# Attention and ternary feed-forward in one kernel: the values by seven products, the chains in twos, two row normalisations on ScalarE, and an earlier decision between paths

## The chip, the cores and the metric

The program runs on one core of a Trainium2 chip. The metric is the time of one execution on the device in microseconds: 1585.0 us as the median of three runs (1584.58 to 1585.37) for the kernel before.

## The reference: what is computed

The input x has 8 sequences of 512 tokens with 256 features, all in f32. Two layers follow each other, each added to its input.

```python
x = x + layernorm(attention(layernorm(x)))
x = x + layernorm(ffn(layernorm(x)))

# attention: 16 heads of 64
q = l2norm(heads(x @ w_q)) * exp(scale)
k = l2norm(heads(x @ w_kv[:, :1024]))
v = heads(x @ w_kv[:, 1024:])
out = merge(softmax(q @ k.T) @ v) @ w_out + b_out

# feed-forward: w1, w2: 256 -> 1024, h1, h2: 1024 -> 1024, w3: 1024 -> 256, entries -1, 0 or 1
h = silu((x @ w1.T) * s1) * ((x @ w2.T) * s2)
h = gelu((h @ h1.T) * hs1)
h = gelu((h @ h2.T) * hs2)
y = (h @ w3.T) * s3
```

## The kernel before

**Order.** Nothing is issued as it is written. Every piece of work is a step with an engine, an estimated length, what it reads and writes and which buffers it takes (`Steps.add`, line 54). `Steps.issue` (line 84) then plays the steps through: TensorE's steps keep the order in which they were added, and each other engine (VectorE, ScalarE, GpSimd, SyncE with its DMA queue) takes, of the steps that are ready by the estimates, the one with the earliest due time. The outcome is the fixed instruction order of every engine. One such plan covers attention, a second one the feed-forward part. On the chip each engine runs its list in order and waits at whatever is not ready.

**Attention.** A batch (one sequence) has 16 heads in two halves of 8 (`hf`), and 8 units, one for each pair of heads. A unit makes four score steps (`scores`, line 728: keys on partitions, two heads at once in the upper and lower rows of the array), eight exponentials on ScalarE, three sums of the exponentials over key blocks on VectorE (`summed`, tile `es`), and four value steps (`values`, line 782, tile `po`, the two heads in the two column halves). The value steps of a unit run after the scores of that unit and before those of the next. For two units together, `row_sums` (tile `pd`) gives the softmax denominators, which go through a fold, a reciprocal and a spread by DMA (`inverted_two`, line 847) before VectorE scales the outputs `oT`.

**Projections beside the units.** The queries, keys and values of the next batch or half are made between the units. The string list `BESIDE` (line 974) has one entry for each of the 8 units: c is a link of a q or k chain, v a value step, x the normalisation and transposes of 128 rows of the next batch, t the sums of token halves, q and k the norm products, m the key norms' transposes, o one output projection, l the store and reload of rows. The products of these stand in TensorE's order between a unit's scores and the next unit's values (q and k ahead of the scores).

A *v step* (`v_step`, line 714, by `projected`, line 400) multiplies 128 tokens by 512 columns of the value weights in two products (two blocks of 128 input features), and ScalarE copies the result to the tile `v`. Four of them make a half.

A *chain* (`qk_chain`, line 518) makes a half of q or k with seven quarter products in place of eight, by the Strassen-Winograd scheme over (2 feature blocks) x (2 halves of 256 columns) x (2 halves of 256 tokens). Its seven links are one product pair each: `product` adds two 256-wide matmuls, `kept` copies a running sum out of its PSUM bank on ScalarE, `added` adds a bank into the tile on VectorE, and `squared` makes the squares for the norms. Links share three banks, so a link that goes on adding in a bank waits until that bank's earlier sum was read. The sums of weight quarters are made once (`qk_weight_sums`, line 482), those of tokens once a batch (`token_sums`, line 498). Batch 0 has all its projections made directly at the start (`qk_step`, `v_step`).

**The weight check.** The fast path is right only if the feed-forward weights are -1, 0 or 1 and the score bound holds. During attention, `looked_at` (line 1077) loads weight rows of 1024 columns into the pool `wp` (two buffers) and VectorE marks and gathers deviations into the tile `loose`, 512 columns at a time; `weight_sums` (line 1114) makes four sums of weight blocks for the square layers and stores them to DRAM. `at(...)` in line 1166 names the slots (two for each unit) where this work is added.

**Feed-forward.** Batches go in pairs through `gated`, two square layers (`square`, line 1479, seven products of quarter size with the activations split in two parts) and `ffn_out` (line 1599). There each 128 rows y are scaled, get mean and variance on VectorE, a power on GpSimd (`power`, line 313), are normalised and added to x1 on VectorE (`added`, line 1641), and stored. The rows y live in the pool `rows`, four buffers of the tag a. The first batch's rows get the same treatment at the start in `norm_in` (line 338).

**The decision.** Lines 1715 to 1723, after all steps, reduce `loose` and the bound to one number by a small product over the partitions (tile `pm_bits`), and all engines load it; a nonzero value starts a second, slower program (`tile_row_softmax`). With these inputs it isn't run.

## Time and profile before

| What | Value |
|---|---|
| Median of three runs | 1585.0 us |
| The profiled execution's own time | 1584.32 us |
| Its span, first to last instruction | 1582.5 us |
| Mean granted TensorE clock | 0.998 |
| TensorE busy with matmuls | 1564.5 us (99%) |
| VectorE, ScalarE, GpSimd busy | 1059.5, 917.6, 486.6 us |
| Products of the v steps (line 407) | 256 records, 120.6 us busy |
| Links of the q and k chains (line 539) | 784 records |
| First projection of batch 0 (line 433) begins | 8.23 us |
| First scores (line 738) begin | 55.22 us |
| Last product of the output layer ends | 1571.63 us |
| Last add on VectorE (line 1645) | 1575.93 to 1576.36 us |

All views come from one profiled execution, with times from its span's start. A group's line names the source line, the engine, the operation, the tiles it writes and reads, its shape and count, then the busy time, the mean duration in ns and the engine's idle time before it with what ended it. A line of the timeline has start, duration, engine and line; the count behind x is of merged instructions. Matmuls overlap by a little, so the distance between two starts is what a piece of work costs. Attention ends and the feed-forward part begins at about 980 us.

### The profile page before, as it was taken

The page shows a single profiled execution, that of the slowest core. Times are in us where ns is not written, and L with a number is a line of the kernel's source. Part 1 is how long each engine was busy: PE and PEld are TensorE (multiplying, and loading weights), DVE is VectorE, ACT ScalarE, POOL GpSimd, SP SyncE. Part 2 cuts the span into 40 slices and gives each one's busy share as a digit, 9 for nine tenths or more (in the row PEclk, how much of TensorE's full clock was granted, in tenths as well). Part 3 has the DMA queues.
Part 4 walks back from the last instruction along what each step waited for, and adds up shares of the span by engine and source line. Part 5 has one row for each costly group of instructions (what it writes and reads, how often), then busy time and mean ns, then how long its engine had stood idle before and what let it go on. Part 6 is the DMA issues. An engine that isn't in the chain of part 4 may idle for free.

```text
span 1582.5 us, 19689 instructions
## 1 busy us (share of the span) xinstructions
PE 1564.5 (99%) x7208; PEld 996.6 (63%) x7208; DVE 1059.5 (67%) x1772; ACT 917.6 (58%) x1543; POOL 486.6 (31%) x354
## 2 busy tenths in 40 slices
PE   9999999999999999999999999999999999999997
PEld 4344554554554554554554546788888888888886
DVE  4577776786654553554544557869877886879686
ACT  4666556556556556555555553666466636655662
POOL 4212122122221221321221211554165235625451
PEclk9999999999999999999999999999999999999999
DMA  6233433342220220220221313344324523451540
GB/s 178 65 97 102 120 82 109 121 115 76 54 62 15 58 65 15 58 62 18 58 64 43 85 38 88 111 142 156 121 80 133 171 69 107 146 152 49 160 133 29
DMA packets 77829, 142.66 MB, mean 90 GB/s; under 512 B 18844, under 2 KB 34460, under 8 KB 73628
## 3 DMA queue, kind: packets, MB, share of 16 engines
q1 hardware_dynamic: 58140, 78.40, 17.9%
q0 software_dynamic: 18880, 61.87, 12.5%
q8 instruction: 58, 0.95, 0.3%
q10 hardware_dynamic: 704, 1.05, 0.2%
q14 instruction: 47, 0.39, 0.1%
HBM read 123.49 MB, written 17.29 MB: 89 GB/s over the span
## 4 chain that ended last, share of the span: by engine, by line
PE 96%; DVE 2%; DMA 1%; ACT 0%; issue 0%; POOL 0%; SPq 0%; DVEq 0%
PE g L1494 26%; PE s L738 15%; PE po L792 14%; PE pa L914 7%; PE vp L407 7%; PE p L1420 6%; PE g_q L539 5%; PE g_k L539 5%; PE py L1608 4%; PE pd L816 2%; PE pn_q L627 1%; PE pn_k L627 1%; PE kp L433 1%; PE qp L433 1%; PE pk L698 0%; DMA spread_q<-nq 0%
## 5 line engine op out<-in xcount | busy, mean ns | idle before, releaser
L749 ACT ACTIVATE e<-s,kn 128x512 f32<-128x512 f32 x512 | 306.7, 702 | 96.6 <-PE s L738 96.6
L738 PE MATMUL s<-qT,kT 64*128 64x512 f32 x1024 | 237.1, 602 | 0.0
L1494 PE MATMUL g<-h,wb_S 128*128 128x512 f32 x1024 | 234.3, 389 | 0.0
L792 PE MATMUL po<-e,v 128*64 128x512 f32 x1024 | 233.9, 598 | 0.0
L1494 PEld LDWEIGHTS g<-h,wb_S 128*128 128x128 f32 x1024 | 192.0, 188 | 39.8
L738 PEld LDWEIGHTS s<-qT,kT 64*128 64x128 f32 x1024 | 93.6, 186 | 143.2 <-issue 125.7
L1494 PE MATMUL g<-h,wb_A 128*128 128x512 f32 x768 | 176.4, 389 | 0.0
L314 POOL TENSOR_TENSOR kn<-kn,neghalf 128x32 f32<-128x32 f32 x16 | 87.5, 5468 | 285.8 <-DVE kn L702 285.8
L772 DVE TENSOR_TENSOR es<-es,e 128x1024 f32<-128x1024 f32 x128 | 156.8, 1225 | 24.9 <-ACT e L749 14.0
L1494 PEld LDWEIGHTS g<-h,wb_A 128*128 128x128 f32 x768 | 144.0, 188 | 29.7
L792 PEld LDWEIGHTS po<-e,v 128*64 128x64 f32 x1024 | 69.4, 136 | 139.7 <-issue 131.1
L1312 DVE TENSOR_TENSOR h<-C,h 128x512 fp32r<-128x512 f32 x112 | 129.4, 1211 | 3.9 <-ACT h L1302 3.8
L314 POOL TENSOR_TENSOR nf_q<-nf_q,neghalf 128x32 f32<-128x32 f32 x16 | 87.3, 5456 | 144.9 <-DVE nf_q L661 144.9
L772 DVE TENSOR_TENSOR es<-e,e 128x1024 f32<-128x1024 f32 x64 | 78.3, 1224 | 72.2 <-ACT e L749 71.9
L1312 DVE TENSOR_TENSOR h<-B,h 128x512 fp32r<-128x512 f32 x112 | 107.8, 1001 | 27.1 <-ACT h L1302 26.7
L407 PE MATMUL vp<-wv_sb,aT 128*128 128x512 f32 x256 | 120.6, 599 | 0.0
L914 PE MATMUL pa<-wo_sb,oT 128*128 128x256 f32 x512 | 116.5, 381 | 0.0
L1550 POOL TENSOR_TENSOR B<-B,B 128x512 f32<-128x512 f32 x64 | 102.0, 1621 | 38.9 <-DVE B L1451 34.0
L914 PEld LDWEIGHTS pa<-wo_sb,oT 128*128 128x128 f32 x512 | 95.8, 190 | 20.0 <-ACT e L749 6.1
L888 ACT COPY oT<-po 128x512 f32<-128x512 f32 x64 | 37.4, 584 | 120.2 <-PE po L792 118.2
L878 DVE RECIPROCAL fold<-fold 128x16 f32<-128x16 f32 x31 | 7.8, 252 | 147.0 <-DMA fold<-d 147.0
L1550 POOL TENSOR_TENSOR C<-C,C 128x512 f32<-128x512 f32 x64 | 94.0, 1495 | 27.7 <-DVE h L1312 27.2
(170 smaller groups left out, 2320.8 us busy)
## 6 DMA issues: line engine op xcount, KB each, us to landing
wb_S<-s POOLq DMA_DIRECT2D x32, 1024.0 KB, 5.1
spread_q<-nq SPq DMA_DIRECT2D x32, 512.0 KB
rden<-r SPq DMA_DIRECT2D x62, 256.0 KB
wb_A<-in_h1T_dram POOLq DMA_DIRECT2D x12, 1024.0 KB, 5.6
wb_A<-in_h2T_dram POOLq DMA_DIRECT2D x12, 1024.0 KB, 5.6
s<-w SPq DMA_DIRECT2D x32, 256.0 KB
w<-in_h1T_dram SPq DMA_DIRECT2D x8, 512.0 KB
x<-xres SPq DMA_DIRECT2D x32, 128.0 KB
```

The source lines that it names most:

```text
L314: nc.gpsimd.tensor_tensor(d, d, neghalf.to_broadcast([P, n]), ALU.pow)
L407: nc.tensor.matmul(pm, lhsT=T["aT", b][:, c, ts(t, P)], rhs=w[:, c, c0 : c0 + HALF], start=(c == 0), stop=(c == ND - 1),)
L539: nc.tensor.matmul(T[key][:, o, :], lhsT=w[:, ts(o, P)], rhs=rhs, start=(fresh and o == 0), stop=True, skip_group_check=True,)
L738: nc.tensor.matmul(tile_of(ps_w, [P, S], tags[h], ss[h]), lhsT=T[kT][hp, j, ts(jb, P)], rhs=T[qT][hp, j, :], start=True, stop=True,)
L749: nc.scalar.activation(T[e][:, h, :], T[ss[h]], AF.Exp, scale=T["kn", b, hf][:, jb, 2 * j + h : 2 * j + h + 1],)
L772: nc.vector.tensor_tensor(T[t], T["e", b, p, 0] if jb == 1 else T[t], T["e", b, p, jb], ALU.add)
L792: nc.tensor.matmul(T[po][h * DH : (h + 1) * DH, :], lhsT=T[v][:, jb, c0 : c0 + DH], rhs=T[e][:, h, :], start=(jb == 0), stop=(jb == NT - 1),)
L914: nc.tensor.matmul(T[pm], lhsT=T["oT", b, p][:, ts(t, P)], rhs=wo_sb[:, p, :], start=(p == 0), stop=(p == NP - 1),)
L1312: lambda: nc.vector.tensor_tensor(T[h][:, 1, c, :], T[raw][:, c, :], T[h][:, 0, c, :], ALU.subtract),
L1420: nc.tensor.matmul(T[ps[k]], lhsT=(w1r, w2r)[k][c][:, ts(o, P)], rhs=row_halves(b, i)[0][:, c, :], start=(c == 0 and i == 0), stop=(c == N ...
L1494: nc.tensor.matmul(T[to[o]], lhsT=T[w][:, c, ts(o, P)], rhs=T[h][:, i, c, :], start=(first and c == 0 and i == 0), stop=(c == NQ - 1 and i ...
L1550: lambda: (nc.gpsimd if T_ENGINE == "pool" else nc.vector).tensor_tensor(T[dst][:, c, :], T[x][:, c, :], T[y][:, c, :], ALU.subtract),
```

## The change

The values of batches 1 to 7 are made by the same seven-product chains as q and k: `qk_chain` becomes `qkv_chain`, where a chain for v has the tokens as the stationary operand and the weights as the moving one, keeps four sums by ScalarE and adds three by VectorE, and makes no squares. The weight sums exist for v too, and are now made after the direct projections of batch 0, whose value products read the weights that they overwrite.

`BESIDE` deals chains out in twos: in unit 0 the k chain (d) and the v chain of the second half alternate link by link, in unit 2 the q chain (c) and the k chain of the next batch's first half, in unit 6 its second half's q chain and first half's v chain. The links' order within a chain changes (the sixth after the third, the fourth after the fifth). Units 3, 4, 5 and 7 have no links.

The weight check works on 256 columns at a time, with one load buffer in place of two and loads and stores of half the width; weight blocks come in 16 pieces of two loads each.

The rows of batch 0 at the start and those of the last two batches at the end are normalised by an Identity activation on ScalarE, with a bias that VectorE makes first; the last rows y stand in one buffer of the pool `blockp` in place of four in `rows`. The decision's instructions become steps that are added ahead of the last pair's square layers.

```diff
-    wp = attn_scope.enter_context(tc.tile_pool(name="wp", bufs=2))
+    wp = attn_scope.enter_context(tc.tile_pool(name="wp", bufs=1))
...
+        if (kind, b) == ("a", 0):
+
+            nb = ("nb", *n)
+
+            def bias():
+                tile_of(small, [P, 1], "nb", nb)
+                nc.vector.scalar_tensor_tensor(
+                    T[nb], T[mv][:, 0:1], -1.0, T[rs], ALU.mult, ALU.mult
+                )
+
+            def normed_rows():
+                tile_of(rows, [P, D], "a", xn)
+                nc.scalar.activation(T[xn], T[x][:, t, :], AF.Identity, bias=T[nb], scale=T[rs])
+
+            steps.add("dve", 0.15, bias, reads=[(rs, 0)], writes=[(nb, 0)], takes=[("nb", 4, nb)])
+        steps.add(
+            "act" if (kind, b) == ("a", 0) else "dve", 0.42, normed_rows,
+            reads=[(x, t), (rs, 0), (("nb", *n), 0)], writes=[(xn, 0)], takes=[("a", 4, xn)],
...
+    wsum = qksum.tile([P, 6, 3, 2 * P], F32, name="wsum")
     HS = S // 2
 
     def quarter(which, hf, k):
-        w = wq_sb if which == "q" else wk_sb
+        w = {"q": wq_sb, "k": wk_sb, "v": wv_sb}[which]
         if k[0] == "A" or k == "S3":
             i, j = (1, 0) if k == "S3" else (int(k[1]) - 1, int(k[2]) - 1)
             return w[:, j, hf * HALF + i * HS : hf * HALF + (i + 1) * HS]
-        return wsum[:, "qk".index(which) * 2 + hf, "S1 S2 S4".split().index(k), :]
-
-    def qk_weight_sums(which, hf):
+        return wsum[:, "qkv".index(which) * 2 + hf, "S1 S2 S4".split().index(k), :]
+
+    def qkv_weight_sums(which, hf):
...
+    def qkv_chain(b, hf, which):
 
 
         n = (which, b, hf)
         to, sq, t = (which + "T", b, hf), ("spread", *n), ("tsum", b)
+        if which == "v":
+            to = ("v", b, hf)
...
+                    x_, y = (rhs, w) if which == "v" else (w, rhs)
                     nc.tensor.matmul(
-                        T[key][:, o, :], lhsT=w[:, ts(o, P)], rhs=rhs,
+                        T[key][:, o, :], lhsT=x_[:, ts(o, P)], rhs=y,
...
         def part(i, k):
+            if which == "v":
+                i, k = k, i
             return T[to][:, 2 * i : 2 * i + 2, ts(k, HS)]
+
+        own = "v" if which == "v" else which + "T"
...
+            if which == "v":
+                return
...
         def fourth():
             added(0, 1, product(3, "S4", "B22", 1, False, last=True))
+            squared(0)
 
         def fifth():
             added(1, 1, product(7, "S3", "T3", 0, False))
 
         def sixth():
             added(0, 0, product(2, "A12", "B21", 2, True, last=True))
-            squared(0)
 
         def seventh():
             kept(1, 0, product(4, "A22", "T4", 0, False, last=True))
             squared(1)
 
-        return [first, second, third, fourth, sixth, fifth, seventh]
+        return [first, second, third, sixth, fifth, fourth, seventh]
...
+            "pe", 0.86, products, reads=[(e, 0), (e, 1), (v, jb), *((v, ("c", i, jb // 2)) for i in range(2))],
+            writes=[(po, 0)],
...
-        "c c v c c c c v c x x x x",
+        "d v d v d v d v d v d v d v x x x x",
         "k o m o t",
-        "c c o c c c c o c",
-        "q v v l",
-        "c c v c c c c v c",
-        "k v",
-        "c c m c c c c v c",
+        "c d o c d o c d c d c d c d c d",
+        "q k l",
+        "m",
+        "",
+        "c v c v c v c v c v c v c v",
         "q",
...
-    loose = const.tile([P, S], I32, name="loose")
+    STRIP = 256
+    loose = const.tile([P, STRIP], I32, name="loose")
...
+            for c0, rows_of in loads:
+                shape = rows_of.shape[1:]
+                d = dst[:, c0 : c0 + shape[0] * (shape[1] if len(shape) > 1 else 1)]
+                nc.sync.dma_start(
+                    d if len(shape) == 1 else d.rearrange("p (c n) -> p c n", n=shape[1]), rows_of
+                )
...
+            "sync", 0.1 * len(loads), load, lag=9.0, writes=[(w, i) for i in range(4)],
+            takes=[("wrows", 1, w)], earliest=after,
+        )
+        for i in range(4):
...
+                "dve", 0.38, lambda i=i: marked(i), reads=[(w, i)], writes=[(y, 0)],
                 takes=[("y", 1, y)],
             )
             steps.add(
-                "dve", 0.72, lambda i=i: gathered(i), reads=[(y, 0)], writes=[("loose", 0)]
+                "dve", 0.38, lambda i=i: gathered(i), reads=[(y, 0)], writes=[("loose", 0)]
...
+        w = looked_at(
+            n, (k, c),
+            [
+                (
+                    2 * i * STRIP,
+                    w_rows[:, k + i * NH // 2, :].rearrange("p (h n) -> p h n", h=2)[
+                        :, :, ts(c, STRIP)
+                    ],
+                )
+                for i in range(2)
+            ],
+            after,
...
+                lambda: nc.sync.dma_start(sums_dram[n, j][:, k, ts(c, STRIP)], part(into)),
...
-        at(8 + 10 * i if i < NH else 56 + 4 * i, work)
+        at(8 + 4 * i, work)
...
-    for hf in range(2):
-        for w in "qk":
-            qk_weight_sums(w, hf)
...
+    for hf in range(2):
+        for w in "qkv":
+            qkv_weight_sums(w, hf)
...
+            last = b // 2 == B // 2 - 1
...
+                if not last:
+                    tile_of(rows, [P, D], "a", y)
+                else:
+
+                    k = b % 2 * NT + t
+                    if ylast not in T:
+                        tile_of(blockp, [P, NQ, S], "b", ylast)
+                    T[y] = T[ylast].rearrange("p a s -> p (a s)")[:, ts(k, D)]
                 nc.vector.tensor_tensor(T[y], T[pys[t]], s3_sb, ALU.mult)
...
+            def bias():
+                nc.vector.scalar_tensor_tensor(
+                    T[mv][:, 0:1], T[mv][:, 0:1], -1.0, T[rs], ALU.mult, ALU.mult
+                )
...
+            takes = [("a", 4, y)]
+            if last:
+                takes = [("b", 7, ylast)] if (b % 2, t) == (1, 0) else ()
+            steps.add(
+                "dve", 0.42, scaled, reads=[(pys[t], 0)], writes=[(y, 0)], takes=takes
             )
...
+            if last:
+
+                steps.add("dve", 0.15, bias, reads=[(rs, 0)], writes=[(nb, 0)])
+                steps.add(
+                    "act", 0.4,
+                    lambda: nc.scalar.activation(T[y], T[y], AF.Identity, bias=T[mv][:, 0:1], scale=T[rs]),
+                    reads=[(rs, 0), (nb, 0)], writes=[(y, 0)],
+                )
+            steps.add(
+                "dve", 0.43 if last else 0.84, added, reads=[(rs, 0), (x, t)], writes=[(y, 0)]
+            )
 
...
+    bits = const.tile([P, 2], F32, name="bits")
+
+    def which_path():
+
+        pm = ("pm_bits", 0)
+
+        def seen():
+            nc.vector.tensor_scalar(loose, loose, 0x7FFFFFFF, None, ALU.bitwise_and)
+            nc.vector.tensor_reduce(bits[:, 0:1], loose, AX.X, ALU.max)
+
+        def both():
+            nc.vector.tensor_copy(bits[:, 1:2], over)
+            nc.vector.tensor_tensor(bits[:, 0:1], bits[:, 0:1], bits[:, 1:2], ALU.add)
+
+        def products():
+            bank(0, pm)
+            nc.tensor.matmul(T[pm][:DH, 0:1], lhsT=ones, rhs=bits[:, 0:1], start=True, stop=True)
+
+        def decided():
+            nc.vector.tensor_scalar(over[:DH], T[pm][:DH, 0:1], 0.5, None, ALU.is_gt)
+
+        steps.add("dve", 1.0, seen, writes=[("bits", 0)])
+        steps.add("dve", 0.2, both, writes=[("bits", 0)])
+        steps.add("pe", 0.06, products, reads=[("bits", 0)], writes=[(pm, 0)], takes=[(0, 4, pm)])
+        steps.add("dve", 0.1, decided, reads=[(pm, 0)], writes=[("over", 0)])
...
+        if n == B // 2 - 1:
+            which_path()
...
-    nc.vector.tensor_scalar(loose, loose, 0x7FFFFFFF, None, ALU.bitwise_and)
-    bits = const.tile([P, 2], F32, name="bits")
-    nc.vector.tensor_reduce(bits[:, 0:1], loose, AX.X, ALU.max)
-    nc.vector.tensor_copy(bits[:, 1:2], over)
-    nc.vector.tensor_tensor(bits[:, 0:1], bits[:, 0:1], bits[:, 1:2], ALU.add)
-    pm = banks[0].tile([P, S], F32, tag="g", name="pm_bits")
-    nc.tensor.matmul(pm[:DH, 0:1], lhsT=ones, rhs=bits[:, 0:1], start=True, stop=True)
-    nc.vector.tensor_scalar(over[:DH], pm[:DH, 0:1], 0.5, None, ALU.is_gt)
```

## The prediction

> **What bounds the kernel now.** I read the page first (busy times, the chain that ended last), then TensorE's timeline in one batch, then the places where it is not back to back, and last the groups of the engines that get work.
>
> ```profile
> span 1582.5 us, 19689 instructions
> ...
> PE 1564.5 (99%) x7208; PEld 996.6 (63%) x7208; DVE 1059.5 (67%) x1772; ACT 917.6 (58%) x1543; POOL 486.6 (31%) x354
> ...
> PE 96%; DVE 2%; DMA 1%; ACT 0%; issue 0%; POOL 0%; SPq 0%; DVEq 0%
> ```
>
> The chain of waits is TensorE's own work for 96% of the span. Since ends of matmuls are modelled, I take durations from one start to the next. An f32 product leaves two records. Batch 5, timeline of TensorE (start, duration, line, tile, records):
>
> ```profile
> 697.53 3.70 PE L407 MATMUL vp<-wv_sb,aT 128*128 128x512 f32 x8
> 701.16 3.65 PE L792 MATMUL po<-e,v 128*64 128x512 f32 x16
> 704.75 3.70 PE L738 MATMUL s<-qT,kT 64*128 64x512 f32 x16
> 708.38 1.13 PE L539 MATMUL g_k<-aT,wk_sb 128*128 128x256 f32 x4
> 709.35 1.03 PE L539 MATMUL g_k<-tsum,wsum 128*128 128x256 f32 x4
> 710.21 1.88 PE L407 MATMUL vp<-wv_sb,aT 128*128 128x512 f32 x4
> 711.93 1.03 PE L539 MATMUL g_k<-tsum,wsum 128*128 128x256 f32 x4
> 712.79 1.03 PE L539 MATMUL g_k<-aT,wsum 128*128 128x256 f32 x4
> ```
>
> A v step (two 512-wide products) lasts 710.21 to 711.93 = 1.72 us, a chain link (two 256-wide ones) 711.93 to 712.79 = 0.86; there is no hole between them. The pair of v steps that stands alone takes 3.63 (697.53 to 701.16) in place of 3.44: 0.19 go at its two edges, where products over the whole array meet those over row or column halves. I found such edges everywhere, and nearly no waits: of the batch's 120 us (629.11 to 749.17) every piece is one of these. One exception, a chain of batch 1 run in batch 0 with nothing between its links:
>
> ```profile
> 84.84 1.13 PE L539 MATMUL g_q<-tsum,wsum 128*128 128x256 f32 x4 [0.21 <-ACT qT L560]
> ...
> 89.34 1.13 PE L539 MATMUL g_q<-tsum,wq_sb 128*128 128x256 f32 x4 [0.78 <-DVE qT L570]
> 90.40 3.65 PE L792 MATMUL po<-e,v 128*64 128x512 f32 x16
> ```
>
> From 82.63 to 90.40 it takes 7.77 where other chains take 7 x 0.86 + 0.2 = 6.24. From 980 us on, the feed-forward part shows no hole to its last product, so what TensorE is spared shortens the span one for one, as long as nobody new makes it wait. The tail, timeline of the last engines:
>
> ```profile
> 1571.88 0.15 DVE L1722 TENSOR_SCALAR over<-pm_bits 64x1 int32<-64x1 f32 x1 [0.56 <-PE pm_bits L1721]
> 1571.95 0.41 DVE L1631 TENSOR_TENSOR y<-py,s_sb 128x256 f32<-128x256 f32 x1
> ...
> 1573.14 0.40 DVE L1642 TENSOR_SCALAR y<-y,ymv,yrs 128x256 f32<-128x256 f32 x1
> ...
> 1575.93 0.43 DVE L1645 TENSOR_TENSOR y<-y,x1r 128x256 f32<-128x256 f32 x1
> ```
>
> The last product ends at 1571.63, VectorE's last add at 1576.36: 4.73 us, of which 3.22 (1573.14 to 1576.36) are four rows' normalise and add in a row. After it come the store's landing and the closing barriers, 6.1 us that the change leaves alone. VectorE's groups and its load in the second and fifth batch (windows: us, then busy time of PE, PEld, DVE, ACT, POOL):
>
> ```profile
> L570 DVE TENSOR_TENSOR kT<-g_k,kT 128x512 f32<-128x512 f32 x42 | 27.9, 687 | 8.4 <-PE g_k L539 7.7
> L1090 DVE SCALAR_TENSOR_TENSOR y<-w 128x512 f32<-128x512 f32 x44 | 30.2, 686 | 0.6
> L509 DVE TENSOR_TENSOR tsum<-aT 128x256 f32<-128x256 f32 x14 | 5.9, 420 | 7.6 <-ACT aT L368 7.6
> 235.00:355.00 120.00, 120.00 (x545) 62.66 (x544) 88.71 (x149) 70.00 (x117) 27.14 (x12) 1.00 0.39 113
> 629.11:749.17 120.06, 120.06 (x548) 62.66 (x544) 62.20 (x106) 69.67 (x116) 26.59 (x12) 1.00 0.18 46
> ```
>
> **The change, part by part.** *Seven products for the values.* Fourteen halves (batches 1 to 7, two each) swap 4 v steps x 1.72 = 6.88 us for 7 links x 0.86 = 6.02: 14 x 0.86 = 12.0 us off TensorE. That a link costs half a v step is the g row's price; the values' links have the same shape with the two operands' places changed.
>
> *Chains in twos.* I price it by the segment that stands between scores and values in each of the eight units of a batch. Batches 1 to 6, before: 10.55, 7.55, 13.15, 3.63, 9.68, 1.91, 8.45, 0 = 54.92 us. After: unit 0 has 14 links, the four transposes and edges, 12.06 + 0.97 + 0.1 = 13.13; unit 1 is as it was, 7.55; unit 2 gains 7 links, 13.15 + 6.03 = 19.18; unit 4 keeps key transposes alone, 0.44 + 0.2 = 0.64; unit 6 is 12.06 + 0.2 = 12.26; units 3, 5, 7 nothing: 52.76. That is -2.16 a batch (1.72 of it the values), -13.0 for six. Batch 0: 7.77 + 9.68 + 1.91 + 8.45 = 27.81 before, 12.26 + 0.64 + 12.26 = 25.16 after, -2.65, since the exposed chain gets a partner. Batch 7: 9.67 + 3.63 before, 12.26 after, -1.04. Together **-16.7 us**: 12.0 values, 1.5 the exposed waits, 3.2 edges of segments that vanish. The norm products of q and k that move together (0.97 and about 0.88) cost the same as apart.
>
> *What makes a link wait.* The seventh link uses the bank that VectorE reads for the fifth's sum. Cover before: one link (0.86) where the chain was bare, and the wait was 0.78; a v step (1.72) elsewhere, and none. After: three links, 2.58, against 0.17 + 0.69 for the sum, so 1.7 us of slack for VectorE's queue, which holds sums of e at 1.22 each. I take 0; with two such ahead, up to 0.7 a chain. ScalarE's copies have the same 2.58.
>
> *VectorE's load.* 14 x 3 sums of 0.686 = 28.8 us, off the path while it is idle: in the fifth batch 58 of 120 us are free, in the second 31, and the values add 4.1. The weight check goes from 120 instructions (82.4 us in the rows L1090, L1095, L1127) to 240 of half the width; at the 0.39 spacing of the 256-wide tsum rows that is 94, at their 0.42 duration 101. So +12 to +19, in the first 500 us, where no product waits for it. Eight more weight sums of 0.42 fall in the first 60 us, when VectorE is half idle. Uncovered, all of this is 44 us.
>
> The row says that a 512-wide sum out of PSUM takes 0.69 and lies beside products. The Trainium skill, page "Trainium Kernel Development and Optimization", section Best Practices, warns to mind PSUM pressure, since packing TensorE speeds up compute but not the emptying of PSUM, and the change empties seven products where it emptied four. By that rule, with the 28.8 us exposed, the gain would become a loss of about 12 us, 1597; by the idle time in the windows it is hidden.
>
> *SP's queue.* Check loads and stores go from 22 + 32 issues to 38 + 64 of 0.3 to 0.6 us each, ahead of the denominators' and norms' transfers. One buffer in place of two means a chunk's load waits for the last chunk's stores. The needs behind it are far: a q norm has from unit 3 to unit 7's scores, over 40 us. I take 0; upper end one 0.6 us issue in each of 31 pairs that it could hold up, 19, were that cover gone.
>
> *Bare units.* Units 3 to 5 lose the products beside them. A bare unit is 3.63 + 3.58, ScalarE's eight exponentials 4.73 plus a 0.59 copy; at 71.78 to 79.00 two halves follow with no hole. At the end of batch 7, though, one row sum takes 1.31 for 1.00 and the next values 3.92 for 3.58. Batch 7's unit 3 now is bare too: I add two such, +0.6, bounds 0 to 0.3 x 3 x 7 = 6.3.
>
> *First rows.* VectorE sheds four normalisations (0.41) for four biases (0.15), ScalarE gets them at its 0.37 to 0.39 copy price with a hop more. The first projection (8.23 us) stands behind the fourth row's transposes, whose power now ends some 0.3 earlier but passes two engines more: 0, between -0.5 and +0.5.
>
> *Last rows.* After the last product: scale, stats, power as before to about 1573.9; then bias 0.15, ScalarE 0.4, add 0.43 with hops of 0.1: about 1575.1 against 1576.36, the other rows' adds fitting in the waits. **-1.2**, between -1.6 and 0. A table load for the new function would cost 1.28 (the ACT_TABLE_LOAD rows' mean) and eat it; the trace shows copies between Gelu calls without one. The Trainium skill, page "ScalarE: Activation LUTs", section "Table sets: the hidden batching unit", says that identity is in every set; by it nothing is loaded, and the term stays -1.2.
>
> *Decision ahead.* Its product (0.22) and compare (0.15) leave the tail; one such product goes into TensorE's order before the last square layers, waiting for VectorE work that is ready long before. Net +0.1, up to +0.5.
>
> Sum: -16.7 + 0.6 - 1.2 + 0.1 = -17.2. The profiled execution took 1584.32 (span 1582.5 and 1.8 around it): 1567.1. The median of the runs, 1585.0, lies 0.7 above it: **1567.8 us**.
>
> **Rivals.** (1) *VectorE falls behind while it checks weights*, batches 1 to 4: 89 of 120 us become about 98 of 118. For it: strict order on that engine, and 27 idle stretches that wait for a fold's landing. Against: no product of batch 2 waits at 89. If half of the 24 chains there lose the 0.7: 8 us, 1576. (2) *The bare units stall* as at batch 7's end: 6.3 us, 1573.5. Against: in batch 0 bare units ran without a hole. (3) *The other side: the seventh link waits for the fifth's sum in all 42 chains*, since both chains' sums now come in one stretch with the sums of e. The price is 0.86 at full exposure, 36 us, 1604; from 17.2 / 42 = 0.41 a chain on, the kernel is slower. For it: 0.78 in the bare chain. Against: 2.58 of cover. (4) *The change doesn't do what it says at the tail*: stats and power alone set the end, and the -1.2 does not come: 1569.
>
> **How the numbers follow.** Forecast 0.70, with its own range of 1566 to 1570, since each small term moves it by about 1; (4) 0.06; (1) 0.10; (2) 0.07; (3) 0.06; 0.01 for less. The range is 1565.5 to 1575: it takes (4), (2) and the smaller half of (1). Left out are (3), half of (1) and some 0.03 below. What a measurement of this kernel can tell from no change is about 0.2%, 3.2 us: faster than 1581.8 are the forecast, (4), (2), (1) and a little of (3), 0.92; within it 0.03; slower 0.05.
>
> **What the new profile would show.** Links of the values' tile at 0.86 start to start; about 100 us fewer v-step products and 84 more link time; a batch of about 117.9 us; no wait of a product for VectorE's sums; segments of 12.3 in unit 6; the last add 3.4 to 3.7 us after the last product, with no table load there. I am wrong if products wait for qT, kT or v on VectorE, if pd waits for es in units 3 to 5, or if the first projection starts later than 8.7 us.

## The result and the profile after

The changed kernel takes 1576.22 us (median of 5 runs, 1575.33 to 1578.65), the kernel before 1584.58 (1582.56 to 1585.37) beside it. The ratio is 0.9953, with an interval of 0.9942 to 0.9964: 8.4 us faster. The forecast was 17.2 us and a range of 1565.5 to 1575.0, so the direction was right and the time was missed: half of the gain isn't there. The five runs go with the mean TensorE clock that was granted: 1575.33 and 1575.38 at 0.999, 1576.22 (the profiled one) at 0.997, 1577.46 and 1578.65 at 0.996.

The page of the profiled execution (1576.22 us, its span 1574.4):

```profile
span 1574.4 us, 20329 instructions
...
PE 1556.7 (99%) x7376; PEld 1034.0 (66%) x7376; DVE 1099.5 (70%) x1942; ACT 919.8 (58%) x1555; POOL 484.1 (31%) x354
...
PE 95%; DVE 2%; DMA 1%; issue 0%; ACT 0%; SPq 0%; POOL 0%; POOLq 0%; DVEq 0%; ACTq 0%
```

TensorE still sets the end, for 95% of the chain in place of 96. The products of the values do what they should. TensorE's timeline in unit 6 of batch 1 (start, duration, line, tile, records):

```profile
257.52 1.03 PE L558 MATMUL g_q<-aT,wsum 128*128 128x256 f32 x4
258.39 1.03 PE L558 MATMUL g_v<-wsum,aT 128*128 128x256 f32 x4
259.25 1.03 PE L558 MATMUL g_q<-tsum,wq_sb 128*128 128x256 f32 x4
260.12 1.03 PE L558 MATMUL g_v<-wv_sb,tsum 128*128 128x256 f32 x4
261.07 3.65 PE L817 MATMUL po<-e,v 128*64 128x512 f32 x16
```

A link of q or of the values takes 0.86 us from start to start, the seventh of each chain among them (the last two), and the whole segment 248.79 to 261.07 = 12.28, where I had 12.3. What is new stands in the waits of TensorE:

```profile
PE pd L842 <- DVE es L797: 3.4, 2, 2.3
...
PE p L1463 <- DVE fh L1443: 1.2, 1, 1.2
PE pt_a L363 <- ACT xn_a L394: 0.8, 3, 0.4
```

The row sums (pd) wait for VectorE's sums of e. The largest holes are batch 4's and batch 7's. Batch 4, units 4 and 5, first VectorE, then TensorE (start, duration, ..., idle before and what ended it; ... stands for lines left out):

```profile
582.03 2.55 DVE L797 TENSOR_TENSOR es<-es,e 128x1024 f32<-128x1024 f32 x2
586.00 0.69 DVE L924 TENSOR_TENSOR oT<-oT,rden 128x512 f32<-128x512 f32 x1 [1.42 <-DMA rden<-r]
...
587.36 0.42 DVE L1118 SCALAR_TENSOR_TENSOR y<-w 128x256 f32<-128x256 f32 x1
...
589.65 0.42 DVE L1123 SCALAR_TENSOR_TENSOR loose<-y,loose 128x256 int32<-128x256 int32 x1
590.00 1.22 DVE L797 TENSOR_TENSOR es<-e,e 128x1024 f32<-128x1024 f32 x1
591.32 2.56 DVE L797 TENSOR_TENSOR es<-es,e 128x1024 f32<-128x1024 f32 x2
```

```profile
588.26 3.65 PE L817 MATMUL po<-e,v 128*64 128x512 f32 x16
591.85 1.05 PE L842 MATMUL pd<-es,ones 128*32 128x512 f32 x4
593.93 1.05 PE L842 MATMUL pd<-es,ones 128*32 128x512 f32 x4 [1.03 <-DVE es L797]
```

VectorE takes its instructions in their written order. It stands idle for 1.42 us for the spread reciprocals (rden, asked for at 581.35), does that multiplication and six instructions of the weight check, and only then sums unit 5's exponentials; ScalarE had made the last of them at 589.93. The second half of the row sum starts 2.08 after the first. The Trainium skill says it as a rule in "PSUM — Partial Sum Buffer", section "Engine vs sequencer instructions": the queues of ScalarE, VectorE and GpSimd are strictly first in, first out. The rows above agree with it.

Batch 7's hole has a second part. Its row sum, the scores after it, and TensorE's window behind the hole (the third-last figure is the granted clock, 0.50); last, the same scores in the trace of the last experiment below, where the same wait was 3.25 us and the clock stayed at 1.00:

```profile
936.38 1.12 PE L842 MATMUL pd<-es,ones 128*32 128x512 f32 x4 [2.34 <-DVE es L797]
937.42 5.29 PE L763 MATMUL s<-qT,kT 64*128 64x512 f32 x16
```

```profile
937.23:940.64 3.41, 3.41 (x10) 1.52 (x10) 0.25 (x1) 1.69 (x3) 0.00 (x0) 0.50 0.02 2
```

```profile
937.99 3.70 PE L763 MATMUL s<-qT,kT 64*128 64x512 f32 x16
```

The scores take 5.29 us in place of 3.70 and wait for nothing: the clock was halved for 3.41 us.

Where the time between the first scores and the first gated product went, by TensorE's tiles. I take each run of records of one tile from its start to the next tile's start, and call excess what it takes over its records at the median price (0.2158 us for a record of a link, 0.4292 of a v step, 0.1104 of a row sum, 0.2240 of values, 0.2271 of scores):

| us | Stretch | q, k links | values' products | row sums (pd) | values (po) | scores | others |
|---|---|---|---|---|---|---|---|
| before | 924.5 | 7.0 | 4.0 | 1.8 | 0.4 | 0.0 | 0.5 |
| after | 917.0 | 3.0 | 1.0 | 9.5 | 2.0 | 1.6 | 0.8 |

At these prices 224 records of v steps (96.1 us) became 392 of links (84.6): -11.6. The excess at links and v steps, edges and waits, fell by 7.0. Row sums, values and scores gave 10.9 back (the scores' 1.6 of it by the halved clock), others 0.3. Together -7.4, and the stretch is 7.5 shorter. The rest of the span: the first scores come at 55.81 in place of 55.22 (+0.6); from the first gated product to the last product 593.4 in place of 591.9 (+1.5); the last add 3.43 after the last product in place of 4.72 (-1.3); from it to the end 4.8 in place of 6.1 (-1.3).

### The profile page after: what moved, and what is told of

Read it like the earlier page. It is cut to its first block, busy times and chain, and to the rows that moved or that the text cites. A ratio compares the mean times of both kernels' runs of the same rounds, so it can differ in the third digit from the quotient of the medians.

```text
span 1574.4 us, 20329 instructions
## 1 busy us (share of the span) xinstructions
PE 1556.7 (99%) x7376; PEld 1034.0 (66%) x7376; DVE 1099.5 (70%) x1942; ACT 919.8 (58%) x1555; POOL 484.1 (31%) x354
## 4 chain that ended last, share of the span: by engine, by line
PE 95%; DVE 2%; DMA 1%; issue 0%; ACT 0%; SPq 0%; POOL 0%; POOLq 0%; DVEq 0%; ACTq 0%
PE g L1537 26%; PE s L763 14%; PE po L817 14%; PE p L1463 7%; PE pa L940 7%; PE g_q L558 5%; PE g_v L558 5%; PE g_k L558 5%; PE py L1652 4%; PE pd L842 2%; PE vp L422 1%; PE kp L448 1%; PE qp L448 1%; PE pn_q L652 1%; PE pn_k L652 1%; DVE es L797 1%
## 5 line engine op out<-in xcount | busy, mean ns | idle before, releaser
L817 PE MATMUL po<-e,v 128*64 128x512 f32 x1024 | 235.8, 599 | 0.0
L797 DVE TENSOR_TENSOR es<-es,e 128x1024 f32<-128x1024 f32 x128 | 156.8, 1225 | 17.6 <-ACT e L774 6.5
L314 POOL TENSOR_TENSOR ors<-ors,neghalf 128x1 f32<-128x1 f32 x32 | 19.2, 600 | 262.7 <-DVE kn L727 163.9
L1584 DVE TENSOR_TENSOR C<-g,C 128x512 f32<-128x512 f32 x96 | 65.2, 687 | 45.1 <-PE g L1537 45.1
L1562 ACT ACTIVATE C<-C,hs_sb 128x512 f32<-128x512 f32 x96 | 68.6, 722 | 47.7 <-DVE C L1584 47.5
```

Source lines behind the costliest of these rows:

```text
L314: nc.gpsimd.tensor_tensor(d, d, neghalf.to_broadcast([P, n]), ALU.pow)
L797: nc.vector.tensor_tensor(T[t], T["e", b, p, 0] if jb == 1 else T[t], T["e", b, p, jb], ALU.add)
L817: nc.tensor.matmul(T[po][h * DH : (h + 1) * DH, :], lhsT=T[v][:, jb, c0 : c0 + DH], rhs=T[e][:, h, :], start=(jb == 0), stop=(jb == NT - 1),)
L1562: nc.scalar.activation(T[dst][:, o, :], x, AF.Gelu, scale=s[:, f : f + 1])
```

## The experiments

Ratios are to the kernel before on the same chip, whose medians there were 1584.2 to 1584.3. Diffs are against the changed kernel. The stretch is always that from the first scores to the first gated product.

**Theories** on the 10.9. A: units 3 to 5 have no links any more, so that VectorE's sums, behind a wait in its fixed order, are not covered. B: VectorE has too much work. C: ScalarE's order delays exponentials. D: VectorE and ScalarE together bound these units, and waits only change place.

### Cover for unit 4

```diff
-        "c d o c d o c d c d c d c d c d",
-        "q k l",
-        "m",
-        "",
-        "c v c v c v c v c v c v c v",
+        "c c o c c c o c c",
+        "q l",
+        "d v d v d v d v d v d v d v",
+        "k",
+        "c c c c c m c c",
```

> The changed kernel (1576.2 us) with its links dealt out otherwise, nothing else: unit 2 keeps q's seven links and two output projections, k's and the values' fourteen lie in unit 4 in place of the key transposes alone, k's norm products move to unit 5 and the key transposes into unit 6 among q's seven. The same products, copies and sums are done. Theory A (thin cover: with units 3, 4 and 5 without links, the values of unit 4 wait for exponentials and the row sums of unit 5 for sums of e, which stand behind a transfer on VectorE): in batches 0 to 6 these waits go, 0.28 for the values and up to 2 us for the row sums a batch, while batch 7 keeps its own (it has no links of a next batch to move): 1570 to 1573. Theory B (VectorE has too much work since it sums the values' products and checks weights in twice as many instructions): its work is unchanged, so 1576 within 1.

1579.1 us (1578.99 to 1580.46), ratio 0.9971 (0.9959 to 0.9983): slower than the changed kernel, against both theories' numbers. The waits named by A did go: row sums 9.5 to 4.1, values 2.0 to 0.3, and with them the halved clock, scores 1.6 to 0, in all 8.7 us. But the excess of the q and k links rose from 3.0 to 13.9. Most of it lies where q's chains now run without a partner: 0.67 in the first five links of each of the seven in unit 6, for ScalarE's copies and at the edges, and 1.48 in the one with nothing beside it in batch 0. Three pairs of k and the values have 0.7 to 1.7 besides (unit 4 of batch 0, unit 0 of batches 4 and 7). So the loss in bare units is real, and this way of covering them costs more than it saves.

### Longer figures for the transfers

```diff
-            takes=[("fold", 1, f)], lag=1.8,
+            takes=[("fold", 1, f)], lag=4.0,
...
-            writes=[(r, c) for c in range(2)], takes=[("rden", 1, r)], lag=4.0,
+            writes=[(r, c) for c in range(2)], takes=[("rden", 1, r)], lag=7.0,
```

> The changed kernel with only the planner's figures for the denominators' transfers longer (the fold's landing 4.0 in place of 1.8, the spread's 7.0 in place of 4.0), so that VectorE's written order puts sums of e ahead of the multiplication that waits for the spread reciprocals. Theory A, in the form that the order on VectorE is the cause: the waits of row sums for es (7.7 us in the three largest groups of the chain of waits, 4.7 of it in batches 4 and 7) shrink by most, the 3.86 of the values in unit 4 stays: 1571 to 1574. If the sums are late because the exponentials are late (ScalarE, theory C), the order on VectorE does not matter: 1576 within 1. Theory B: 1576 within 1.

1585.12 us (1583.62 to 1589.36), ratio 1.0008 (0.9999 to 1.0017): no faster than the kernel before. The sums of e of unit 5 now stand ahead of the multiplication in all eight batches, and the row sums' excess fell from 9.5 to 2.6, as A said. Something else appeared, once in each of batches 0 to 6:

```profile
105.95 1.13 PE L763 MATMUL s<-qT,kT 64*128 64x512 f32 x4 [1.32 <-ACT nd_k L676]
```

The scores' excess went to 11.2, seven times 1.59. With longer figures the planner sets ScalarE's copy of k's norms behind four exponentials rather than one. It takes one of two buffers of the pool `sqp` that the folds read, and until it has run, its PSUM bank is not free for the last scores. The links lost another 4.9.

### Without the check's instructions

```diff
-        for i in range(4):
-            y = ("y", n, k, i)
-            steps.add(
-                "dve", 0.38, lambda i=i: marked(i), reads=[(w, i)], writes=[(y, 0)],
-                takes=[("y", 1, y)],
-            )
-            steps.add(
-                "dve", 0.38, lambda i=i: gathered(i), reads=[(y, 0)], writes=[("loose", 0)]
-            )
         return w
```

> The changed kernel without the two VectorE instructions per strip that look for zeros and denormals in the weights (240 instructions, about 95 us of VectorE's busy time); loads, weight sums and stores stay. So the kernel no longer finds out which path the weights need. Theory B: the lost 8.6 us of the attention come back, 1567 to 1570. Theory A: only the waits in which check instructions stand ahead of sums of e (batch 4's 2 us, a little elsewhere) go, those behind the spread reciprocals stay: 1573 to 1576.

1580.98 us median (1577.64 to 1582.58), ratio 0.998 (0.9971 to 0.999); its stretch takes 917.0, what the changed kernel's takes. The edit takes away 176 instructions and 64.9 us of VectorE's busy time (1099.5 to 1034.6), not the 240 and 95 expected. The 8.6 us that B promised don't come, so B falls. The row sums' excess fell by 4.3, as A says where check instructions stand ahead, and the scores' by 1.6, since the clock wasn't halved; that of the q and k links rose by 5.4, in chains of unit 0. (The profiled execution, whose stretch this is, took 1577.77.) VectorE in batch 2, unit 0, then the link that waits:

```profile
284.69 0.69 DVE L593 TENSOR_TENSOR kT<-g_k,kT 128x512 f32<-128x512 f32 x1 [0.24 <-PE g_k L558]
289.12 0.69 DVE L709 TENSOR_TENSOR qT<-qT,spread_q 128x512 f32<-128x512 f32 x1 [3.74 <-DMA spread_q<-nq]
289.73 0.68 DVE L593 TENSOR_TENSOR v<-g_v,v 128x512 f32<-128x512 f32 x1
```

```profile
290.47 1.13 PE L558 MATMUL g_v<-wv_sb,tsum 128*128 128x256 f32 x4 [2.43 <-DVE v L593]
```

VectorE is idle for 3.74 us with a link's sum next in line: my third rival's wait, made by order and not by load.

### The chains in twos alone

```diff
...
-        "d v d v d v d v d v d v d v x x x x",
+        "d v d d v d d v d d v d x x x x",
...
-        "c v c v c v c v c v c v c v",
+        "c v c c v c c v c c v",
...
-        v = [(b, lambda b=b, hf=hf, k=k: link(b, hf, "v", k)) for b, hf in v for k in range(7)]
+        v = [(b, lambda b=b, hf=hf, t=t: v_step(b, hf, t)) for b, hf in v for t in range(NT)]
```

> The changed kernel with the values by four 1.72 us steps a half again, dealt out among the same units as the links were, all else as changed: the order of the chains in twos without the seven products. The prediction's term of 12.0 us for the values, if right beside everything else: 1588.2 (14 halves x 0.86 more than the changed kernel). If the values' sums and copies cost time where they stand, the term is smaller, 1580 to 1585. Theory A adds that it is then slower than the kernel before (1584.6), since the bare units are there without the gain of the products.

In this kernel the difference S3 still replaces a quarter of the values' weights, so its values are not the reference's; the instructions and their sizes are those of v steps. 1587.25 us (1585.4 to 1589.24), ratio 1.0016 (1.0007 to 1.0025): slower than before, as A adds. The stretch is 928.0. So dealing the chains out in twos makes it 3.5 longer (from 924.5: row sums +3.8, values +1.9, links and v steps -2.5), and the seven products make it 11.0 shorter (to 917.0), 1587.25 to 1576.22 and 1576.83 in the runs. (This trace too has 3.41 us at half the clock, from 383.27 on, behind a link that waited 2.39 us; by half of 3.41, an estimate, 1.7 of the 3.5 are the clock's.) The term of 12.0 was about right; the edges' gain was more than eaten.

### The changed kernel again, and the copy of k's norms

> The changed kernel once more, beside the next three on the same chip: 1576 within 1.5 for every theory, with the same 7 values of 3.86 in unit 4 and the same row sums of 1.55, 2.17, 3.07 and 4.43 in unit 5, since the order is written out.

1576.83 us (1575.36 to 1577.11), ratio 0.9952 (0.9937 to 0.9967), with the same holes: +0.67, +1.45, +2.22 and +4.49 over a row sum's price at 117, 236, 592 and 933 us, and seven values of 3.86.

```diff
-        "q k l",
-        "m",
-        "",
+        "q l",
+        "k",
+        "m",
```

> The changed kernel with k's norm products moved from unit 3 to unit 4 and the key transposes from unit 4 to unit 5, so that ScalarE's copy of k's norms no longer stands between the exponentials of unit 4. Theory C (the values' 3.86 come from that copy, 0.59 in the middle of eight exponentials, on ScalarE): the seven 0.28 go, 2.0 us, less an edge of some 0.1 for each of seven norm products that now stand alone, 0.7: 1574.5 to 1575.5; the row sums in unit 5 keep their waits. If they come from the order on VectorE, nothing changes, 1576 to 1577.

1575.07 us (1574.23 to 1575.88), ratio 0.9945 (0.9932 to 0.9959). Unit 4 of batch 0 on ScalarE, in the changed kernel and then here:

```profile
102.92 0.69 ACT L774 ACTIVATE e<-s,kn 128x512 f32<-128x512 f32 x1 [1.36 <-PE s L763]
103.51 0.58 ACT L676 COPY nd_k<-pn_k 128x512 f32<-128x512 f32 x1
103.97 4.17 ACT L774 ACTIVATE e<-s,kn 128x512 f32<-128x512 f32 x7
```

```profile
102.08 4.73 ACT L774 ACTIVATE e<-s,kn 128x512 f32<-128x512 f32 x8 [0.50 <-PE s L763]
108.22 0.59 ACT L914 COPY oT<-po 128x512 f32<-128x512 f32 x1 [1.41 <-PE po L817]
109.25 0.58 ACT L676 COPY nd_k<-pn_k 128x512 f32<-128x512 f32 x1 [0.45 <-PE pn_k L652]
```

ScalarE had been idle 1.36 us ahead of that copy's place, but the copy came in the middle of the exponentials. Moved, the seven 0.28 are gone, as C says (values' excess 2.3 to 0.3); the row sums keep theirs (9.6).

### The copy and the longer figures together

This is the edit of `BESIDE` just shown with the two lags of the second experiment.

> As the run before, and with the planner's figures for the denominators' landings at 4.0 and 7.0 as in the second experiment, so that sums of e stand ahead of the multiplication in VectorE's order. The second experiment took 7 us of row-sum waits away and got 9.6 us of waits of the scores in unit 4 instead, which all lie behind the copy of k's norms (set behind four exponentials, while it holds a bank that the scores need). Theory A+C: with the copy out of the way both waits go, 7 for the row sums, 1.6 for what followed in batch 7, 2.0 for the values, less 0.7 of edges and some 3 for sums of links in unit 0 that wait as they did in the second experiment: 1567 to 1572. If waits only move to another place whatever the order (theory D, VectorE and ScalarE together are the bound of these units): 1575 to 1580.

1584.73 us (1582.4 to 1587.17), ratio 1.0005 (0.9996 to 1.0014). The scores' waits are gone (0.0), the row sums' excess is 4.8, but that of the values' links is 11.9, the largest hole in unit 6 of batch 0 (4.46, q's and the values' together, some 1.5 of it at half the clock). There VectorE stood 7.57 us for q's spread norms, to 125.29, was then busy without a pause beyond 141, and the links' sums came behind weight sums at 139.74. Two figures redraw the whole order; every redrawn order had a wait somewhere else. Up to here D could stand.

### The first rows on VectorE again

```diff
-        if (kind, b) == ("a", 0):
+        if False:
...
-            "act" if (kind, b) == ("a", 0) else "dve", 0.42, normed_rows,
+            "act" if False else "dve", 0.42, normed_rows,
```

> The changed kernel with the first batch's rows normalised on VectorE again. The activation with a bias and a scale for each partition took 0.60 us in the changed kernel's profile, VectorE's normalisation 0.41 before; the first projection stood at 8.75 against 8.23 us and the first scores at 55.81 against 55.22. If this edit is all of the difference at the head: first scores at 55.2 and 0.6 us less, 1575.6. If the head's 0.6 is due to something else, for instance the eight weight sums for the values, the first scores stay at 55.8.

1575.5 us (1573.57 to 1578.38), ratio 0.9951 (0.9938 to 0.9965); the runs' spread is wider than the effect, but the profile is plain: first projection 8.28, first scores 55.27 in place of 55.81. The head's 0.6 is this edit. The changed kernel's rows there:

```profile
5.76 0.60 ACT L394 ACTIVATE xn_a<-xres,nb_a,rs_a 128x256 f32<-128x256 f32 x1 [1.63 <-DVE nb_a L388]
6.57 1.09 ACT L394 ACTIVATE xn_a<-xres,nb_a,rs_a 128x256 f32<-128x256 f32 x2 [0.21 <-DVE nb_a L388]
```

### One edge more in VectorE's order

```diff
+        if u[1] == 5:
+            for p in (2, 3):
+                normalised(u[0], p, behind=[(("es", *u), 0)])
         for jb in range(NT):
             values(*u, jb)
...
-        elif p % 2:
+        elif p % 2 and p != 3:
             normalised(b, p - 1)
             normalised(b, p)
```

Here `behind` is added to the reads of the multiplication's step.

> The changed kernel with one edge more in VectorE's order and nothing else: the multiplication of units 2 and 3 by their spread reciprocals is set behind the sums of e of unit 5 of the same batch. No figure of a transfer is changed, so the rest of the order stays. Theory A (the row sums of unit 5 wait because these sums stand behind a multiplication that waits for a transfer): the four waits of row sums (0.67, 1.29, 2.19, 3.55 over a row sum beside other products) fall to at most 0.43 each and batch 7's 1.58 of the scores behind them goes: 6 to 8 us less, 1568.5 to 1571; the values' 0.28 in unit 4 stay. Theory D (VectorE and ScalarE together bound these units, so that waits only change place): 1574 to 1580.

1570.33 us (1569.93 to 1570.55), ratio 0.9915 (0.9901 to 0.9928). The same units of batch 4 as above, on VectorE and TensorE:

```profile
587.27 1.23 DVE L797 TENSOR_TENSOR es<-e,e 128x1024 f32<-128x1024 f32 x1 [2.92 <-ACT e L774]
588.60 2.56 DVE L797 TENSOR_TENSOR es<-es,e 128x1024 f32<-128x1024 f32 x2
591.07 0.18 DVE L727 TENSOR_SCALAR kn<-pk 128x32 f32<-128x32 f32 x1
591.17 1.33 DVE L924 TENSOR_TENSOR oT<-oT,rden 128x512 f32<-128x512 f32 x2
```

```profile
587.88 3.65 PE L817 MATMUL po<-e,v 128*64 128x512 f32 x16
591.46 1.07 PE L842 MATMUL pd<-es,ones 128*32 128x512 f32 x8
592.46 3.70 PE L763 MATMUL s<-qT,kT 64*128 64x512 f32 x16
```

The sums start with the exponentials, the multiplication no longer stands ahead of them, and the row sum takes 1.00. In the view of the tile pd, the idle time ahead of TensorE's row-sum products and their weight loads, which overlap, for the sums of e falls from the first line (the changed kernel) to the second (this one):

```profile
DVE es L797: 13.3, 10
```

```profile
DVE es L797: 2.9, 5
```

The stretch is 910.0, 7.0 shorter; row sums 9.5 to 3.2, scores 1.6 to 0.0, links +0.7. Batch 0's 0.67 stayed (0.72). TensorE's and ScalarE's orders are the changed kernel's, VectorE's differs for about 100 of 1942 instructions. So A is shown, and D is not the bound that it seemed to be: with the same work on both engines the waits are gone. 1.6 of the 7.0 is the clock, which isn't halved here; against the last experiment's stretch, 916.2 with batch 7's hole and a full clock, the gain is 6.2.

### All of it together

The edge, the later norms of k and the first rows on VectorE, and SP's reload moved:

```diff
-        "q k l",
-        "m",
-        "",
+        "q",
+        "k",
+        "m l",
```

> The edge of the run before, k's norms a unit later as in the sixth experiment, the first rows on VectorE as in the eighth, and the reload of the residual rows moved from unit 3 to unit 5 on SP, so that it no longer stands ahead of the fold in batch 7. Theory A+C: the gains add: 6 to 8 for the row sums, 1.3 for the values, 0.7 for the head, nothing to 1 for the reload: 1566 to 1569, about what the prediction named for the change itself. Theory D: 1573 to 1578.

1569.99 us (1569.76 to 1570.32), ratio 0.9913 (0.9899 to 0.9926): it beats both kernels, but not the edge alone by more than these runs tell apart. The head came (first scores 55.24) and the values' excess went (0.5), but row sums have 5.8 in place of 3.2, eight of them at +0.43 or more. They come due earlier: the key transposes, which stood between the scores and the values of unit 5 (587.29 to 587.88 in the edge's run), went a unit on with the norms. What the reload alone does was not separated.

### The last rows and the decision

```diff
-            last = b // 2 == B // 2 - 1
+            last = False
```

> The changed kernel with the last rows normalised on VectorE again, in their old tiles. The prediction's term was 1.2 us: 1577.7, with the last add 4.6 to 4.8 us after the last product in place of 3.4. If the rows' normalise on ScalarE was not what shortened the tail, 1576.5 and 3.4.

1578.63 us (1578.14 to 1580.74), ratio 0.9966 (0.9952 to 0.998): about 2 us slower, more than the term. The last add is 5.93 after the last product in place of 3.43. One wait of it is not the normalisation's:

```profile
1569.32 0.42 DVE L1683 TENSOR_TENSOR y<-py,s_sb 128x256 f32<-128x256 f32 x1 [1.47 <-DMA out_dram<-y]
```

The rows' four buffers are full until a store has read one. Without that wait, 5.93 - 1.47 = 4.46, the tail is about 1.0 longer, near the 1.2 of the prediction; the changed kernel's own tile for all eight last rows avoids the wait as well. (A wait of 0.6 for a transfer in the square layers adds to this run.)

```diff
-        if n == B // 2 - 1:
-            which_path()
...
+    which_path()
     with tc.manual_schedule(engines=ORDERED):
         steps.issue()
```

> The changed kernel with the decision between paths made behind the last square layers again, as the last steps of the planned order. The prediction gave this part +0.1 net: 1576.2 to 1576.8, with its product (0.21 to 0.28) back among the last ones. If what came after the last add (4.8 to 5.2 us in place of 6.1) was shortened by the decision: 1577 to 1578.

1577.44 us (1575.72 to 1579.86), ratio 0.996 (0.9946 to 0.9973). The edit moves the decision's product and compare only: the planner leaves its four VectorE instructions where the changed kernel has them, at the start of the feed-forward part. That part is 0.5 shorter (592.9 for 593.4), so the earlier product costs 0.5 there, its own 0.2 in it. The last add comes 3.43 after the last product as before. From there to the end there are 8.2 us, though, in place of 4.7 to 7.3 in the other runs that keep the changed tail. In this run's trace TensorE's branch over the second program starts at 1568.58, after the last add, and takes 3.70 us, where the other engines' take 0.07 or less.

## Why the prediction was wrong

**Seven products for the values, -12.0: right.** -11.6 at common prices, 11.0 between the stretches with and without them.

**Chains in twos, -3.2 for edges and -1.5 for exposed waits: right, but low.** The excess at links and v steps fell by 7.0, in place of 4.7. The text took one exposed chain for the only exception; the kernel before had a second, a k link that waited 1.1 us for VectorE's sum at 476.9, and its segment took 11.04 us in place of 9.67. That wait went too.

**"What makes a link wait", 0: right for this order.** The seventh link's cover of 2.58 us held: no product of a chain waited, but for some 0.3 in unit 0 of batch 3 (an excess of 0.40 there, 0.11 in most others, which are the edges). Three experiments show how thin it is: with VectorE's order redrawn, the values' links had an excess of up to 11.9 us in sum. Rival 3 didn't come, but its wait exists.

**VectorE's load and SP's queue, 0: the load right, the order wrong.** VectorE's busy time grew by 40.0 us (estimate 44), and without the check's instructions nothing is gained, so rival 1 fell as it was put, although its time, 1576, is the one measured. The text saw "27 idle stretches that wait for a fold's landing" and strict order, and didn't ask what stands behind these waits once the cover is gone. The transfers themselves are not the news: in unit 3, from the fold's issue to the spread's, they took 3.6 to 6.5 us before and 3.6 to 6.9 after.

**"Bare units", +0.6: this is the step that failed.** I priced a bare unit from two rows at batch 7's end, 0.31 and 0.34, and added two such, with 6.3 as the upper bound. It cost 10.9: row sums 7.7, values 1.6, scores 1.6. The row sums' part is VectorE's order (the one edge takes away 6.3), the values' is the copy of k's norms on ScalarE (shown by moving it), the scores' is the halved clock behind batch 7's hole. The rows that I took showed a bare unit in which VectorE's sums happened to be in time. What had to be followed is the round from unit 3's row sums over fold, reciprocal and spread to the multiplication. Batch 7, on ScalarE, SP and VectorE:

```profile
918.69 0.58 ACT L856 COPY d<-pd 128x512 f32<-128x512 f32 x1 [0.43 <-PE pd L842]
```

```profile
921.66 0.59 SPq L884 DMA_DIRECT2D fold<-d  x1
```

```profile
931.23 1.29 DVE L924 TENSOR_TENSOR oT<-oT,rden 128x512 f32<-128x512 f32 x2 [2.48 <-DMA rden<-r]
933.77 2.55 DVE L797 TENSOR_TENSOR es<-es,e 128x1024 f32<-128x1024 f32 x2
```

From the copy of the sums to the multiplication it ran 12.5 us; the multiplication's 1.2 and unit 5's three sums, 3.9, stand behind it in a queue that can't change places, and make 17.6. (2.4 of the 12.5 are SP's: the copy was done at 919.27, and the fold was issued at 921.66, behind the reload of the residual rows; before, that was 0.6. No run takes this alone away.) Unit 5's row sums were due 15.4 us after unit 3's (917.55 to 932.99); before it was 19.0 there (925.3 to 944.3), and 29.6 in batches 1 to 6 (210.4 to 240.0), which now have 18.0 (217.8 to 235.8). A single row sum lost up to 3.55, ten times my price, so the bound fell too. Rival 2 named the place, with the wrong price.

**First rows, 0 within 0.5: wrong, +0.6.** The normalisation on ScalarE takes 0.60, not the 0.37 to 0.39 of a copy of that size. It has a scale and a bias for each partition; that these are the difference fits, but no run here shows it. The Trainium skill, "ScalarE: Activation LUTs", section "What ACT_TABLE_LOAD costs", gives 186 ns + 0.833 ns an element and about 93 ns for each such operand: an estimate of 0.585 for 256 elements and two operands. The trace's 0.60 agrees with it.

**Last rows, -1.2: right.** -1.3 by the last add, which came 3.43 after the last product (3.4 to 3.7 forecast), with no table load there. Rival 4 fell.

**Decision ahead, +0.1 and at most +0.5: too low, about +1.4.** 0.5 is its product, by the last experiment. The rest the text didn't ask for: "VectorE work that is ready long before" stands somewhere in VectorE's order. VectorE ahead of the first pair's lower halves (fh), first the kernel before, then the changed one:

```profile
990.21 1.40 DVE L1451 SCALAR_TENSOR_TENSOR B<-p,s_sb,sg 128x512 f32<-128x512 f32 x2
991.52 0.68 DVE L1400 TENSOR_TENSOR fh<-ptf,fh 128x512 fp32r<-128x512 f32 x1
```

```profile
983.27 0.29 DVE L1754 TENSOR_SCALAR loose<-loose 128x256 int32<-128x256 int32 x1
983.59 0.42 DVE L1755 TENSOR_REDUCE bits<-loose 128x1 f32<-128x256 int32 x1
...
984.59 0.15 DVE L1758 CAST bits<-over 128x1 f32<-128x1 int32 x1
984.77 0.16 DVE L1759 TENSOR_TENSOR bits<-bits 128x1 f32<-128x1 f32 x1
...
985.52 0.68 DVE L1443 TENSOR_TENSOR fh<-ptf,fh 128x512 fp32r<-128x512 f32 x1
```

The kernel before has no such instruction there. The four make fh 0.9 later, and the next fh too, which VectorE reaches without a pause; for that one TensorE waits 1.17 us in place of 0.26. This is read from the order; no run takes the four away.

**Not in the sum.** The end after the last add is 1.3 shorter here, but 4.7 to 7.3 us in other runs with the same tail, so it isn't shown to be the change's. Nor is a halved clock in the sum: 1.6 us in the profiled execution.

**The signs of being wrong.** Two of the three came: pd waited for es in unit 5, and the first projection started at 8.75, later than 8.7. (The chances have a slip: forecast, (4), (2) and (1) alone make 0.93 for "faster", where the text has 0.92.)

-18.6 for products, edges and waits, +10.9 and +0.3 for bare units and others, +0.6, +1.5, -1.3 and -1.3 are -7.9; the spans differ by 8.1. Without the bare units' 10.9 the time would have been about 1565, an estimate, below the forecast by about the 2.3 that edges and waits gave beyond it.

## What to carry to other kernels

When work that covered a stretch is moved away, follow the longest round of transfers that ends in it, and look at what is queued behind the instruction that waits for its landing: the price is that queue's wait, not the price of a bare stretch that happened to be in time. An order written by a planner should be mended by the one edge that is wrong; a changed figure for a transfer redraws every queue and moved the waits elsewhere in both tries. An excess table by tile, at common prices, shows such exchanges (8.7 us gained, 10.9 lost among the links) where the time alone says only "slower"; an excess that waits for nothing should be held against the granted clock.

## What the runs showed of the hardware

Behind a long hole of TensorE the granted clock can fall to 0.50 for 3.41 us. It did so in five of the seven traces in which TensorE once waited 2.3 us or more (2.34 in the changed kernel, 2.39, 2.47, 2.65 and 2.9 in others), not in the other two (2.43 without the check's instructions, 3.25 in the last experiment), and in none of the traces whose waits after the head are 1.8 or less. What decides between the two is not shown.

TensorE's conditional branch over the second program takes 3.3 to 4.2 us in all fourteen traces, the other engines' 0.04 to 0.07. Before the change it began at 1572.66 and ended at 1576.62, just behind the last add; decided early, it runs from 1564.49 on, behind TensorE's last issue; in the last experiment it began after the last add. The time from the last add to the end varies by 2.6 us among runs with one and the same tail.
